# Where seven fill transfers stand on GpSimd in a two-layer cross-attention kernel

## The chip, the cores and the metric

The kernel runs on one core of one Trainium2 chip, in float32. A core has a matrix engine (TensorE, "PE" in the profile), a vector engine (VectorE, "DVE"), a scalar engine (ScalarE, "ACT"), GpSimd ("POOL") and SyncE ("SP"), and 16 DMA engines[...]. The metric is the device time of one execution in microseconds; lower is better. The median of three runs of the kernel before is 599.94 us (597.68 to 600.04).

## The reference

Two cross-attention layers over a batch of 8. The queries `x` have 100 rows of 1024 features per batch, the context has 1444 rows of 512.

```python
# layer 0
Q, K, V = query @ Wq + bq, key @ Wk + bk, key @ Wv + bv
weights = softmax(Q @ K.T / 32, axis=-1)              # over the 1444 context rows
x = query + (weights @ V) @ Wo + bo
# layer 1
q, k, v = x @ Wq + bq, ctx @ Wk + bk, ctx @ Wv + bv
w = softmax(q @ k.T / 32, axis=1)                     # over the 100 query rows
x = w @ v + x
out = (x - mean(x)) * rsqrt(var(x) + 1e-6) * gamma + beta
```

What matters for the change is the last line: `beta` is one row of 1024 numbers, and it is added to each of the 100 rows of each batch.

## The kernel before, in words

The kernel multiplies weights together first (`Wq` with `Wk`, `Wv` with `Wo`), so that the context is used as it comes from memory and never projected. It goes through these stages, in this order on the matrix engine:

1. Eight warm-up products (L111), then `qk0`, the product of layer 0's `Wq` and `Wk` (`weight_products`, L350). It is a Strassen-like scheme: the product is cut in quarters A11 to A22 and B11 to B22, and seven half-size products X, Z, W, Y and three more replace eight. X is A11 by B11, and Z is A12 by B21; both use the weights as loaded. W is A22 by T4, where `T4 = B21 - (B22 - (B12 - B11))` is made on VectorE. Y needs sums S1 and T1. The order on the matrix engine here is X, Z, W, Y and then products added to X.
2. `vo0` (`Wv` with `Wo`), the queries of layer 0, `qk1` (as `qk0`, for layer 1).
3. Layer 0's scores, softmax and weighted context rows, batch by batch (L913, L960), then its projection.
4. The queries of layer 1 and `key_bias_sums`, then layer 1's scores, softmax and weighted rows, its projection with `Wv` (loaded at L1380 into `wv1`), and the normalisation of each batch.

The weights of `qk0` come in eight tiles `qk0_0` to `qk0_7` ("units"), each with 1024 columns of transposed `Wq` and 512 of transposed `Wk`. Their loads are cut in halves and are issued in the order of use (L364 to L376): the two pieces of unit 0 on ScalarE's queue, and then, all on SyncE's queue, the first halves of `Wk` and `Wq` for all units (L368 to L371, 128 and 256 KB each), the second halves of `Wk` (L374, eight of 128 KB), and the second halves of `Wq` (L376, eight of 256 KB, units 4 to 7 first). Then come the loads of `vo0` (L379, L380). In the built program each of SyncE's transfers waits for the one eight places before it to have landed.

For all batches but the last, the result is put together by two kinds of transfers on GpSimd. A first one fills `out[b]` with 100 copies of `beta`'s row, straight from memory to memory (L1378; 400 KB each, seven of them). Much later `normalise` (L1234) makes the rest in a tile `z`, and a transfer that adds (L1247) puts it on top of what the fill left. The last batch doesn't use this.

The order of work is set in three ways. The matrix engine's instructions stand as they are written (`manual_schedule`). SyncE's loads in the batch loops (`loaded_in_order`), some activations and the vector operations with `in_order` are marked with `tc.keep_in_program_order`. All other instructions on the other engines are placed by the framework's scheduler, which may bring an instruction forward if nothing that it needs is missing. The fills read only an input and write only the output, so they need nothing: in the built program of the kernel before they stand right after the memset of `top` (L141), as the last of GpSimd's instructions before the first accumulating transfer of `qk0` (L578), though the source has them after the queries of layer 1.

Lines used further on: L130 (loads of bias columns), L141 (`top`), L166 (the products of `half_steps`), L440 (copies of finished products), L578 (accumulating transfers), L972 (memset in `scores_by_keys`), L1177 (last instruction of `weight_sums`), L185 (sums of `wv1` on GpSimd).

## Time and profile before

| | before |
|---|---|
| median of 3 runs | 599.94 us |
| profiled execution, its own time | 601.68 us |
| span of its instructions | 599.9 us |
| mean granted clock of the matrix engine | 0.991 |
| busy share: PE, DVE, POOL, ACT | 96%, 67%, 22%, 22% |
| moved by DMA | 142.96 MB, 6.14 MB of it written to memory |

How to read the profile: a row of a group names the source line, the engine, the operation, `output<-input` by the program's names (buffer and layer numbers left out, so that `qk0_4` is `qk`), the count, and the durations in microseconds or, where marked, nanoseconds. A time in brackets, as in `[3.49 <-DMA qk<-in_L_xattn_WkT]`, is how long the engine had stood idle before the instruction, and what ended this. In the profile of a window the columns are: start and end, length, then busy time of PE, PEld (weight loads), DVE, ACT and POOL, each with its instruction count in brackets, the granted clock of the matrix engine, the mean busy share of the 16 DMA engines, and GB/s.

### The profile page before, as it was taken

To read this page: it belongs to the slowest core of one execution; us is meant where nothing else is said; L and a number is where in the kernel's file an instruction comes from. 1 tells how busy PE (TensorE), PEld (TensorE's weight loads), DVE (VectorE), ACT (ScalarE), POOL (GpSimd) and SP (SyncE) were. 2 spreads that over 40 slices of the span, in tenths; PEclk is the share of its full clock that TensorE was granted. 3 is DMA by queue.
4 is the path that set the end of the run, shared out by engine and by line. 5 is a ranking of instruction groups with operands and counts; after the bars stand their busy time and mean duration, and the time that the engine had idled before them with its cause. 6 is when DMAs were issued, how large, how long until landed. Compare 5 with 4: busy or idle time off the path is not lost.

```text
span 599.9 us, 17567 instructions
## 1 busy us (share of the span) xinstructions
PE 578.0 (96%) x7470; PEld 498.5 (83%) x7470; DVE 399.7 (67%) x936; ACT 133.3 (22%) x349; POOL 134.9 (22%) x206
## 2 busy tenths in 40 slices
PE   8499999999999999999999999999999999999994
PEld 7378645768889999999998856677999999999992
DVE  1199758988867597284558688695644337664695
ACT  1032232131360002022200000112333203145313
POOL 5011011121120022252221100000931421332052
PEclk9889999999999999999999999999999999999998
DMA  8896998984379999899999201915799998499214
GB/s 253 238 295 136 311 299 216 328 201 99 71 158 323 322 393 357 295 379 364 365 341 296 96 0 63 380 55 162 244 292 334 336 301 294 117 315 320 68 29 83
DMA packets 74313, 142.96 MB, mean 238 GB/s; under 512 B 8572, under 2 KB 30332, under 8 KB 74236
## 3 DMA queue, kind: packets, MB, share of 16 engines
q1 hardware_dynamic: 65790, 117.81, 57.4%
q0 software_dynamic: 8048, 23.57, 18.8%
q8 instruction: 59, 0.97, 0.6%
q10 hardware_dynamic: 398, 0.47, 0.2%
q14 instruction: 18, 0.15, 0.1%
HBM read 124.40 MB, written 6.14 MB: 218 GB/s over the span
## 4 chain that ended last, share of the span: by engine, by line
PE 90%; DMA 4%; issue 2%; POOL 2%; ACT 1%; DVE 0%; SPq 0%; POOLq 0%; DVEq 0%
PE s L960 22%; PE A L913 21%; PE qk_x L166 6%; PE g_x L166 5%; PE o_x L166 5%; DMA qk<-in_L_xattn_WkT 4%; PE vo_x L166 3%; PE o_y L166 3%; PE g_y L166 3%; PE qk_y L166 2%; PE qk_w L166 1%; PE o_w L166 1%; PE o_z L166 1%; PE qk_z L166 1%; PE vo_z L166 1%
## 5 line engine op out<-in xcount | busy, mean ns | idle before, releaser
L913 PE MATMUL A<-w,c 128*64 128x100 f32 (+1 forms) x3072 | 228.1, 249 | 0.4 <-issue 0.4
L913 PEld LDWEIGHTS A<-w,c 128*64 128x64 f32 (+1 forms) x3072 | 200.4, 137 | 1.8 <-issue 1.4
L960 PE MATMUL s<-g0T,cT 128*64 128x100 f32 (+1 forms) x1472 | 113.0, 249 | 2.5 <-issue 2.4
L960 PE MATMUL s<-g1T,cT 128*64 128x100 f32 (+1 forms) x1472 | 113.8, 249 | 0.2 <-issue 0.2
L960 PEld LDWEIGHTS s<-g0T,cT 128*64 128x64 f32 (+1 forms) x1472 | 99.2, 136 | 5.0 <-issue 3.9
L960 PEld LDWEIGHTS s<-g1T,cT 128*64 128x64 f32 (+1 forms) x1472 | 97.1, 136 | 2.1 <-issue 1.6
L1172 POOL TENSOR_TENSOR part<-w 128x500 f32<-128x500 f32 x16 | 26.4, 1652 | 126.3 <-ACT w L1020 61.1
L1152 ACT ACTIVATE w<-w,negmax 128x100 f32<-128x100 f32 x96 | 34.9, 366 | 68.2 <-DVE negmax L99 68.2
L1020 ACT ACTIVATE w<-w 128x400 f32<-128x400 f32 (+2 forms) x32 | 12.0, 443 | 122.2 <-DVE w L99 122.2
L99 DVE SCALAR_TENSOR_TENSOR w<-s,kb 128x400 f32<-128x400 f32 (+2 forms) x32 | 13.9, 464 | 37.0 <-PE s L960 36.8
L99 DVE TENSOR_REDUCE most<-s 128x100 f32<-128x400 f32 (+1 forms) x24 | 12.5, 521 | 38.5 <-PE s L960 38.5
L166 PE MATMUL qk_x<-qk 128*128 128x256 f32 x128 | 30.0, 382 | 0.0
L166 PEld LDWEIGHTS qk_x<-qk 128*128 128x128 f32 x128 | 23.6, 192 | 3.0 <-ACT qk L440 0.2
L166 PE MATMUL qk_z<-qk 128*128 128x256 f32 x64 | 16.3, 409 | 8.0 <-DMA qk<-in_L_xattn_WkT 8.0
L166 PEld LDWEIGHTS qk_z<-qk 128*128 128x128 f32 x64 | 12.9, 206 | 11.0 <-issue 7.8
L972 POOL MEMSET w<- 68x100 f32 x16 | 3.8, 238 | 78.4 <-PE A L913 37.9
L1232 DVE SCALAR_TENSOR_TENSOR z<-vectors,r,z 100x512 f32<-100x512 f32 x16 | 11.4, 744 | 11.5 <-PE z L1230 11.3
L99 DVE TENSOR_TENSOR w<-w,rtotal 128x400 f32<-128x400 f32 (+2 forms) x32 | 18.2, 570 | 1.1
L1152 ACT ACTIVATION_READ_ACCUMULATOR w<-w,negmax 128x1 f32 x96 | 18.0, 188 | 0.0
L1245 ACT ACTIVATE z<-z,rstd 100x1024 f32<-100x1024 f32 x7 | 8.0, 1149 | 44.7 <-POOL rstd L1243 44.7
L578 POOL DMA_DIRECT2D qk_L_xattn_bk<-qk_L_xattn_bk x6 | 5.2, 925 | 56.3 <-ACT qk_L_xattn_bk L583 27.5
L99 DVE TENSOR_TENSOR xT<-xT,o_x 128x400 f32<-128x400 f32 (+1 forms) x32 | 16.0, 541 | 2.7 <-PE o_x L166 2.4
(435 smaller groups left out, 1048.1 us busy)
## 6 DMA issues: line engine op xcount, KB each, us to landing
c<-in_ctx SPq DMA_DIRECT2D x176, 256.0 KB
cT<-in_ctxT SPq DMA_DIRECT2D x96, 176.0 KB
cT<-in_ctxT SPq DMA_DIRECT2D x32, 370.0 KB
cT<-in_ctxT SPq DMA_DIRECT2D x32, 352.0 KB
cT<-in_ctxT SPq DMA_DIRECT2D x32, 194.0 KB
vo<-in_L_xattn_Wo SPq DMA_DIRECT2D x8, 512.0 KB
qk<-in_L_xattn_WqT SPq DMA_DIRECT2D x8, 512.0 KB
qk<-in_L_xattn_WqT SPq DMA_DIRECT2D x15, 256.0 KB
```

Of the source, the lines that this page charges most:

```text
L99: ins = getattr(nc.vector, op)(*args, **kw)
L166: nc.tensor.matmul(banks[n // per][:, n % per * width : (n % per + 1) * width], lhs[i][:, n * P : (n + 1) * P], rhs[i], start=(fresh and i ...
L578: nc.gpsimd.dma_start(out=to, in_=t, accum_op=ALU.add)
L913: nc.tensor.matmul(ps[h * HP : (h + 1) * HP, k * T : (k + 1) * T], c[m // CQ][:r, m % CQ, k * P + h * HP : k * P + (h + 1) * HP], w[:r, m, :],
L960: nc.tensor.matmul(to, cT[k][:, o : o + n], q[:, k, t0 : t0 + T], start=(k == 0 and m % GM == 0), stop=(k == LC - 1 or (k == LC - 2 and no ...
L972: nc.gpsimd.memset(s["w"][:PAD, MC - 1, :], 0.0)
L1020: nc.scalar.activation(rows, rows, AF.Exp)
L1152: nc.scalar.activation(rows[:, i, :], rows[:, i, :], AF.Exp, bias=negmax[:, i : i + 1], accum_out=total[:, i : i + 1])
L1172: add(part, w[:, 0:5, :], w[:, 5:10, :], ALU.add)
L1232: nc.vector.scalar_tensor_tensor(z[:, half], bv1[j][:T], s["r"], ps[:T, :], ALU.mult, ALU.add)
L1245: nc.scalar.activation(z, z, AF.Copy, scale=rstd)
```

## The change

The seven fill transfers are marked to keep their place in the program's order. Nothing is computed differently.

```diff
     run(more)
     vector.in_order = False
     for b in range(B - 1):
-        nc.gpsimd.dma_start(out=out[b], in_=a["L1_xattn_beta"].partition_broadcast(T))
+        rows = a["L1_xattn_beta"].partition_broadcast(T)
+        tc.keep_in_program_order(nc.gpsimd.dma_start(out=out[b], in_=rows))
     wv1 = weights.tile([P, LC, E], F32, tag="w", name="wv1")
     nc.gpsimd.dma_start(out=wv1, in_=a["L1_xattn_Wv"].rearrange("(c p) e -> p c e", p=P))
```

In the built program the seven transfers move, on GpSimd alone, from their place between the memset of `top` (L141) and the first L578 to a place right after the last L1177 of layer 0 (the sums of batch 7) and before the L972 memset of layer 1's batch 0 and the load of `wv1`. All other engines have the same instructions in the same order.

```diff
 L141 Memset top
-L1378 DMACopy out<-in_L_xattn_beta x7
 L578 DMACopy qk_L_xattn_bk<-qk_L_xattn_bk
 ...
 L1177 TensorTensor wsum<-wsum,w
+L1379 DMACopy out<-in_L_xattn_beta x7
 L972 Memset w
-L1380 DMACopy wv<-in_L_xattn_Wv
+L1381 DMACopy wv<-in_L_xattn_Wv
```

## The prediction

> **What bounds the kernel now.** I read the page's chain first, then who the matrix engine waited for, then its timeline where it waited, then the transfers.

> ```profile
> PE 90%; DMA 4%; issue 2%; POOL 2%; ACT 1%; DVE 0%; SPq 0%; POOLq 0%; DVEq 0%
> ...
> PE   8499999999999999999999999999999999999994
> PEclk9889999999999999999999999999999999999998
> ```

> These are the chain that ended last, and the busy and clock rows of the 40 slices of 15 us. The matrix engine sets the time from about 30 us to the end; a 4% share (24 us) is DMA, and only slice 2 (15 to 30 us) has a PE that is half idle. So a shift of its later work to an earlier time should come out at the end in full. The waits of PE:

> ```profile
> PE qk_z L166 <- DMA qk<-in_L_xattn_WkT: 8.0, 3, 3.6
> PE s L960 <- issue: 2.6, 6, 0.7
> PE qk_w L166 <- DVE qk_t L99: 2.1, 1, 2.1
> ```

> All the long ones are in the first product `qk0`. Its timeline from 10 to 32 us:

> ```profile
> 11.75 1.89 PE L166 MATMUL qk_z<-qk 128*128 128x256 f32 x8
> 17.13 1.97 PE L166 MATMUL qk_z<-qk 128*128 128x256 f32 x8 [3.49 <-DMA qk<-in_L_xattn_WkT]
> 22.66 3.38 PE L166 MATMUL qk_z<-qk 128*128 128x256 f32 x8 [3.56 <-DMA qk<-in_L_xattn_WkT]
> 27.00 1.99 PE L166 MATMUL qk_z<-qk 128*128 128x256 f32 x8 [0.96 <-DMA qk<-in_L_xattn_WkT]
> 31.08 1.10 PE L166 MATMUL qk_w<-qk_t,qk 128*128 128x256 f32 x4 [2.09 <-DVE qk_t L99]
> ```

> Each group of eight Z products needs one more unit of the weights, and units 5, 6 and 7 come some 5 us apart: 384 KB per 5 us, under 80 GB/s. The wait for `qk_t` is the same lack one step on: VectorE's first difference started at 27.81 after 18.5 us of waiting for the L374 halves. Who took the bandwidth:

> ```profile
> L1378 POOL DMA_DIRECT2D out<-in_L_xattn_beta x7: 537/544/582, 5.7 to 9.4; - x7
> ...
> DMA to landing us min/median/max: 9.7/14.1/18.1
> ```

> The fills are issued from 5.7 us and the last land near 27 us. The stage's windows (last columns: clock, DMA share, GB/s):

> ```profile
> 2.00:5.65 3.65, 3.65 (x18) 3.51 (x17) 1.23 (x2) 0.95 (x1) 3.56 (x8) 1.00 0.94 306
> 12.00:22.00 10.00, 3.61 (x16) 2.55 (x14) 0.00 (x0) 0.54 (x1) 0.00 (x0) 1.00 0.96 248
> 31.00:38.00 7.00, 6.92 (x24) 5.84 (x25) 7.00 (x14) 3.08 (x3) 0.58 (x1) 0.76 0.96 321
> ```

> Without fills the DMA engines move 306 and 321 GB/s; with them 248 at the same busy share, of which 7 x 0.41 = 2.87 MB are the fills'.

> [...] Here the two idle times of 3.49 and 3.56 us are followed by a clock of 0.50 at 23 to 25 us and at 33 to 35 us. [...]

> **What the removal at the start is worth.** Y begins at 39.75. Dense, 32 products of this shape take 6.91 us (Y itself: 39.75 to 46.66). Z starts at 11.75, so W would start at 18.66 and Y at 25.57: 14.18 us earlier. By parts: idle 3.49 + 3.56 + 0.96 + 2.09 = 10.10; slow clock 3.38 - 1.97 = 1.41 in the third Z group and 8.83 - 7.07 = 1.76 in W; 0.91 is the tail of a group's last product, which is hidden when the next follows.

> Can the loads keep that pace? I take 306 GB/s from 2.0 us, and 2.4 us from the last byte to the wait's end; both are estimates from rows, the second from an accumulating transfer of 256 KB that lands 3.3 us after issue, 0.86 us of which is its bytes. First halves of all units are 8 x 0.393 = 3.15 MB: landed at 2.0 + 10.3 + 2.4 = 14.7, needed for the last Z group at 16.9. With the L374 halves 4.19 MB: 18.1. The first A22 block (unit 4's L376) makes 4.46 MB: 19.0, needed at 18.66, so 0.3 late. The last A22 block, 5.24 MB: 21.5, needed at 23.9. The last of all, 6.29 MB: 25.0, needed as S1's last sum before 30.8.

> VectorE: its first difference could start at 15.1. T4's first piece is ready 1.8 us after the start (27.81 to 29.64 now), at 16.9; the last is held by the 18.1 and about 1.4 us of work, 19.5. Its two additions of Z (0.64 each) follow, and S1's first sum is done near 23, 2.5 us before Y. Now it is done at 36.1, 3.6 us before Y. The cover is thinner, but it is there; without it Y would slip by the missing part alone.

> After Y nothing that sets the pace is tied to the clock on the wall: `vo0`'s loads past two units wait for tiles that the `qk0` products free, and DMA share falls to 0.4 to 0.5 at 45 to 55 us, so the next full stretch of DMA starts earlier by the same amount. Gain: 14.18 - 0.3 = 13.9 us.

> **What the new place costs.** The seven issues take 7 x 0.544 = 3.8 us of GpSimd. Around that place:

> ```profile
> 332.22 0.39 POOL L1177 TENSOR_TENSOR wsum<-wsum,w 36x100 f32<-36x100 f32 x1
> 343.01 0.18 POOL L972 MEMSET w<- 68x100 f32 x1 [10.40 <-issue]
> 370.35 0.83 POOL L1380 DMA_DIRECT2D wv<-in_L_xattn_Wv  x1 [27.16 <-PE o_x L166]
> ```

> Queued behind are the L972 memset and the `wv` load. GpSimd stands idle for 10.4 us before the first and 27.2 us before the second, so the issues cost nothing, and even at 1.5 us each (10.4 / 7) they would not delay the memset. If they did, that tile is next written by layer 1's softmax after its scores, which begin at 403.9. The bytes:

> ```profile
> 335.00:345.00 10.00, 10.00 (x194) 9.11 (x191) 5.65 (x9) 0.00 (x0) 0.18 (x1) 1.00 0.01 3
> 345.00:370.35 25.35, 25.35 (x84) 15.23 (x83) 21.75 (x53) 0.00 (x0) 0.00 (x1) 1.00 0.00 0
> ```

> DMA is idle for 35 us there. The fills need 2.87 MB / 0.3 = 10 us alone, 21 us at the crawl of the start. Ahead of them SyncE's queue ends its prefetch at 331.3 and then waits for buffers until 379.8. The L1247 additions, which need the fills landed, begin at 519.8. Cost between 0 and 0.5 us; I take 0. L578 no longer stands behind the fills, but it waited for ScalarE until 37.4, so this is worth nothing of its own.

> Sum: span 599.9 - 13.9 = 586.0. The profiled execution took 601.68, 1.7 above the median; its span stands at the median, so the same subtraction gives 586.0 for the median.

> **Rivals.**
> - *The weights' own stream becomes the bound.* If the rate without fills stayed at the 242 GB/s of 11.75 to 31.08 us, the first A22 block lands at 2.0 + 18.4 + 2.4 = 22.8, 4.1 late, and such a gap brings the slow clock (1.8) again: gain 14.18 - 5.9 = 8.3, 591.6 us. [...] Against: 306 and 321 GB/s in both windows without fills.
> - *Hidden anyway: SyncE's issue sets the pace.* Its eight L374 issues took 15 us. If that were its own doing, nothing changes: 599.9. Against: each takes 0.33 us at the median, and what it waits for are landings.
> - *Slower: the fills make `wv` late.* `wv` is issued at 370.4 and lands 9.9 us later; GpSimd's sums of it (L185) start at 419.3, and the matrix engine reads it first at 492.8, or 478.9 when shifted. Fills from 318.6 would have to last 478.9 - 9.9 - 318.6 = 150 us, 19 GB/s, before PE waits, 164 us to eat the gain, and 167 us to give 603. They had 134 GB/s (2.87 MB in 21.4 us) in the worst crowd of the kernel.
> - *The change does nothing*: excluded by the built order.

> **How the numbers follow.** Full shift (584.5 to 588) 0.72; partly, the stream bounds (588 to 595) 0.18; more than the dense sum, below 584.5 (a later stage also runs freer) 0.04; no change 0.04; slower 0.02. About 0.5% (3 us) is what a measurement of this kernel can tell from no change. Faster 0.94, same 0.04, slower 0.02. The range 583.0 to 591.6 takes in the partial rival's worked value and a run to run spread of 2 us, and leaves out its worse half and the last two cases.

> **What would show it.** After: no PE idle over 1 us and no clock below 1 before 40 us; Y near 25.6 to 26.2; VectorE's first difference near 15; the fills at about 318.6 in an empty DMA; everything between with its old durations. A gap ahead of W with DMA share 1 is the first rival; a PE wait for DVE there means VectorE's cover was too thin; a Y at 26 but an end later than 588 means that a later stage gave time back.

## The result, and the profile after

The changed kernel takes 592.06 us in the median of 6 runs (589.33 to 593.25), the kernel before, in runs beside it, 598.61 us (596.71 to 600.04, 6 runs). The ratio is 0.9883 with a 95% interval of 0.9848 to 0.9918: faster by about 6.5 us, less than half of the 13.9 us that were predicted.

The profiled execution took 589.33 us with a span of 587.6. Its start looks as predicted. Four rows of PE's timeline from 0 to 50 us, the products X, Z, W and Y, answer to the ones with the four gaps:

```profile
4.64 8.31 PE L166 MATMUL qk_x<-qk 128*128 128x256 f32 x32
12.79 7.07 PE L166 MATMUL qk_z<-qk 128*128 128x256 f32 x32
19.70 7.07 PE L166 MATMUL qk_w<-qk_t,qk 128*128 128x256 f32 x32
26.60 7.07 PE L166 MATMUL qk_y<-qk_s 128*128 128x256 f32 x32
```

No row behind the warm-up products has an idle time in brackets, and Y begins at 26.60 instead of 39.75. The waits of PE over the whole execution, which answer to the ones shown of before:

```profile
PE s L960 <- issue: 1.9, 3, 0.7
PE A L913 <- issue: 1.7, 1, 1.7
```

The waits for the weights are gone, but there is a new one of 1.7 us, put down to "issue", which means that PE waited for nothing that the profile shows. GpSimd's timeline around the new place of the fills (start, busy time, engine, line, operation, tiles, shapes, number; in brackets the idle time before it and what ended it):

```profile
317.12 0.39 POOL L1177 TENSOR_TENSOR wsum<-wsum,w 36x100 f32<-36x100 f32 x1
317.46 3.85 POOL L1379 DMA_DIRECT2D out<-in_L_xattn_beta  x7
329.89 0.18 POOL L972 MEMSET w<- 68x100 f32 x1 [8.58 <-issue]
357.23 0.80 POOL L1381 DMA_DIRECT2D wv<-in_L_xattn_Wv  x1 [27.17 <-PE o_x L166]
```

PE's timeline of the changed kernel in the same stretch (excerpt):

```profile
319.32 7.77 PE L913 MATMUL A<-w,c 128*64 128x100 f32 x175
328.74 1.03 PE L913 MATMUL A<-w,c 128*64 128x100 f32 x17 [1.65 <-issue]
329.88 2.96 PE L166 MATMUL o_x<-A0T,vo 128*128 128x400 f32 x8
332.67 2.85 PE L166 MATMUL o_y<-o_t,o_s 128*128 128x400 f32 x8
```

GpSimd issues the fills in 3.85 us and nothing behind them is late, as predicted. But PE, which is at batch 7's weighted rows (192 matmul records, 8.46 us without a break in the kernel before), stops for 1.65 us with 17 records left, while the fills move.

Another part of the shortfall does not show in this trace: the profiled execution of before, from which the gain was worked out, was a long one. That is taken up below.

### The profile page after: what moved, and what is told of

Same layout as the page of the kernel before. It is cut to its first block, busy times and chain, and to the rows that moved or that the text cites. A ratio compares the mean times of both kernels' runs of the same rounds, so it can differ in the third digit from the quotient of the medians.

```text
span 587.6 us, 17570 instructions
## 1 busy us (share of the span) xinstructions
PE 575.2 (98%) x7470; PEld 497.6 (85%) x7470; DVE 399.6 (68%) x936; ACT 133.3 (23%) x349; POOL 135.0 (23%) x206
## 4 chain that ended last, share of the span: by engine, by line
PE 86%; DMA 6%; SPq 2%; issue 2%; POOL 2%; ACT 1%; DVE 0%; POOLq 0%; DVEq 0%
PE s L960 18%; PE A L913 17%; PE qk_x L166 7%; PE g_x L166 6%; PE o_x L166 5%; PE vo_x L166 4%; DMA cT<-in_ctxT 3%; PE o_y L166 3%; PE g_y L166 3%; DMA c<-in_ctx 3%; PE qk_z L166 2%; PE qk_y L166 2%; SPq L861 2%; PE o_w L166 1%; PE o_z L166 1%
## 5 line engine op out<-in xcount | busy, mean ns | idle before, releaser
L960 PE MATMUL s<-g0T,cT 128*64 128x100 f32 (+1 forms) x1472 | 112.7, 249 | 2.0 <-issue 1.9
L960 PE MATMUL s<-g1T,cT 128*64 128x100 f32 (+1 forms) x1472 | 114.1, 249 | 0.1
L960 PEld LDWEIGHTS s<-g1T,cT 128*64 128x64 f32 (+1 forms) x1472 | 97.7, 136 | 2.6 <-issue 1.8
L960 PEld LDWEIGHTS s<-g0T,cT 128*64 128x64 f32 (+1 forms) x1472 | 96.8, 136 | 3.4 <-issue 2.7
L99 DVE SCALAR_TENSOR_TENSOR w<-s,kb 128x400 f32<-128x400 f32 (+2 forms) x32 | 13.9, 463 | 37.5 <-PE s L960 37.3
L99 DVE TENSOR_REDUCE most<-s 128x100 f32<-128x400 f32 (+1 forms) x24 | 12.5, 520 | 36.5 <-PE s L960 36.5
L166 PE MATMUL qk_x<-qk 128*128 128x256 f32 x128 | 31.0, 392 | 0.0
L166 PEld LDWEIGHTS qk_x<-qk 128*128 128x128 f32 x128 | 24.3, 198 | 3.3 <-ACT qk L440 0.2
L972 POOL MEMSET w<- 68x100 f32 x16 | 3.8, 237 | 75.3 <-PE A L913 36.4
L99 DVE TENSOR_TENSOR w<-w,rtotal 128x400 f32<-128x400 f32 (+2 forms) x32 | 18.3, 570 | 1.1
L1152 ACT ACTIVATION_READ_ACCUMULATOR w<-w,negmax 128x1 f32 x96 | 18.1, 188 | 0.0
L99 DVE TENSOR_TENSOR xT<-xT,o_x 128x400 f32<-128x400 f32 (+1 forms) x32 | 15.9, 538 | 2.8 <-PE o_x L166 2.4
L674 ACT ACTIVATE g1T<-g_x,k 128x400 f32<-128x400 f32 x4 | 2.4, 594 | 61.4 <-PE g_x L166 61.2
L578 POOL DMA_DIRECT2D qk_L_xattn_bk<-qk_L_xattn_bk x6 | 5.2, 922 | 47.8 <-DMA qk_L_xattn_bk<-qk_L_xattn_bk 18.9
L166 PE MATMUL vo_x<-vo 128*128 128x512 f32 x32 | 15.3, 595 | 0.0
```

Of the source, the lines that this page charges most:

```text
L99: ins = getattr(nc.vector, op)(*args, **kw)
L166: nc.tensor.matmul(banks[n // per][:, n % per * width : (n % per + 1) * width], lhs[i][:, n * P : (n + 1) * P], rhs[i], start=(fresh and i ...
L578: nc.gpsimd.dma_start(out=to, in_=t, accum_op=ALU.add)
L960: nc.tensor.matmul(to, cT[k][:, o : o + n], q[:, k, t0 : t0 + T], start=(k == 0 and m % GM == 0), stop=(k == LC - 1 or (k == LC - 2 and no ...
L972: nc.gpsimd.memset(s["w"][:PAD, MC - 1, :], 0.0)
L1152: nc.scalar.activation(rows[:, i, :], rows[:, i, :], AF.Exp, bias=negmax[:, i : i + 1], accum_out=total[:, i : i + 1])
```

## The experiments

The kernel before differs by some us from chip to chip (medians of 598.1, 600.2 and 598.9 us in the three sets of runs below), so ratios compare better than times.

**The same two kernels again, without fills, and with the fills a little later.** The first question was whether the new place costs something, and how much. The changed kernel, two variants of it and the kernel before ran on one chip. The first variant leaves the fills out, so that seven batches of its output lack `beta`. The second holds them back behind a copy of one column that needs the last weighted rows of batch 7. In the cuts from the sources, the first is against the kernel before and the second against the changed kernel.

> The changed kernel once more, for the spread of its times and a second trace. Theory A (the fills at their new place hold up the fetch of the matrix engine's instructions during batch 7's weighted rows[...]): times from 589 to 593 us, and the trace has an idle time of PE put down to issue, of 1 to 5 us, between 318 and 332 us, while the fills move[...]. Theory B (the spread is the start's or the chip's): no such gap, and PE loses its time elsewhere. Theory C (start only, the profile of the kernel before was a slow one): the same times as with no fills at all.

> The changed kernel without the seven fills (the output of seven batches lacks beta; all else is done). Theory A: 586 to 588 us in every run, with little spread, and no PE idle time between 300 and 335 us; the difference to the changed kernel is the price of the new place, 2 to 5 us. Theory B: the same spread and median as the changed kernel, within 1 us. Theory C: the same as the changed kernel.

```diff
-    for b in range(B - 1):
-        rows = a["L1_xattn_beta"].partition_broadcast(T)
-        tc.keep_in_program_order(nc.gpsimd.dma_start(out=out[b], in_=rows))
```

> The changed kernel with the fills held back by about 13 us: a one-column copy on GpSimd that reads the last weighted rows of batch 7 stands before them, so that they run while PE does the long products of the projection. Theory A: as without fills, 586 to 588 us, PE dense from 318 to 345 us although the fills take as long there. Theory B and C: as the changed kernel, 589 to 593 us.

```diff
+    gate = const.tile([P, 1], F32, tag="gate", name="gate")
+    tc.keep_in_program_order(nc.gpsimd.tensor_copy(gate, A0[1][:, LC - 1, GT - 1 : GT]))
     for b in range(B - 1):
```

> The kernel before once more, for a second trace. All theories: 596 to 601 us; PE waits of 8 to 13 us in all before Y, and Y begins at 36 to 40 us. If its time is nearer 597 than 601, the start's loss should be smaller by the same 3 to 4 us[...].

| | median (range), us | ratio to before, interval |
|---|---|---|
| before, all runs on this chip | 598.12 (594.3 to 602.2) | |
| before again | 598.14 (596.18 to 600.01) | 0.9999 (0.9976 to 1.0021) |
| changed | 590.33 (588.84 to 592.35) | 0.9867 (0.9839 to 0.9895) |
| changed, no fills | 587.40 (585.30 to 588.05) | 0.9808 (0.9780 to 0.9837) |
| fills after batch 7's rows | 586.85 (585.93 to 588.48) | 0.9814 (0.9788 to 0.9840) |

So the new place costs 590.33 - 587.40 = 2.9 us (with six runs on each side, uncertain by about 2 us), and 14 us further on the same transfers cost nothing that can be seen: theory A. The second trace of the kernel before has PE waits of 1.55 + 4.60 + 0.77 = 6.9 us ahead of Y, less than the 8 to 13 that were expected; its Y begins at 38.14, as expected. The traces say where the 2.9 us are. PE's timeline in the second trace of the changed kernel:

```profile
317.75 7.77 PE L913 MATMUL A<-w,c 128*64 128x100 f32 x175
327.88 1.27 PE L913 MATMUL A<-w,c 128*64 128x100 f32 x17 [2.36 <-issue]
...
329.42 4.19 PE L166 MATMUL o_x<-A0T,vo 128*128 128x400 f32 x8
```

PE's timeline in the kernel with the fills held back until after batch 7's rows:

```profile
320.97 8.46 PE L913 MATMUL A<-w,c 128*64 128x100 f32 x192
...
329.53 2.95 PE L166 MATMUL o_x<-A0T,vo 128*128 128x400 f32 x8
332.32 2.85 PE L166 MATMUL o_y<-o_t,o_s 128*128 128x400 f32 x8
```

GpSimd's timeline of that kernel:

```profile
331.11 0.59 POOL L1378 COPY gate<-A0T 128x1 f32<-128x1 f32 x1 [1.38 <-DVE A0T L942]
331.64 3.85 POOL L1381 DMA_DIRECT2D out<-in_L_xattn_beta  x7
```

In the second trace of the changed kernel the stop is 2.36 us, at the same place, and the eight o_x records after it take 4.19 us instead of 2.95. The table of windows of that second trace shows a lower clock there (start and end, length, the busy times of PE, PEld, DVE, ACT and POOL, and last the clock, the DMA share and GB/s):

```profile
326.00:330.00 4.00, 2.12 (x22) 1.80 (x23) 0.48 (x1) 0.00 (x0) 0.18 (x1) 0.82 0.90 212
330.00:334.00 4.00, 4.00 (x10) 2.15 (x9) 3.83 (x8) 0.00 (x0) 0.00 (x0) 0.76 0.13 42
```

The clock is 0.82 in the stretch in which the stop ends (at 327.88) and 0.76 in the next. With the fills held back both stretches have 4.00 us of PE and a clock of 1.00.

**What PE stops for.** The profile has two DMA queues of kind "instruction", the larger of them q8 (59 packets, 0.97 MB). The 17 records come close to those of the last block of context rows (16), whose first product has waits in the program, so a wait on data that the profile doesn't name could not be excluded. If PE waits instead for its own instructions to come in (the fetch of theory A; that q8 carries them was at this point the author's guess from its kind), the place must move when instructions are put ahead of all others.

> The changed kernel with twelve tiny products (2 by 2 results) after the warm-up, which put 24 more matmul records into the matrix engine's stream ahead of everything. In both traces of the changed kernel the idle time in batch 7's weighted rows ended with 17 matmul records left of 192, with no wait named. Instruction fetch: the place moves with the stream, so the gap ends with 41 left (17 + 24). A wait on data (the 17 are about those of the last block of context rows, which also has a wait in the program): it stays at 17 or 16. Time within 2 us of the changed kernel's 589 to 593.

```diff
     for _ in range(8):
         nc.tensor.matmul(warm[:, :P], ones, ones, start=True, stop=True)
+    for _ in range(12):
+        nc.tensor.matmul(warm[:2, :2], ones[:, :2], ones[:, :2], start=True, stop=True)
```

The cut is against the changed kernel; each of the twelve products makes two matmul records. It took 591.37 us (2 runs; before on this chip 600.15). PE's timeline in that kernel:

```profile
322.17 6.74 PE L915 MATMUL A<-w,c 128*64 128x100 f32 x151
330.29 2.02 PE L915 MATMUL A<-w,c 128*64 128x100 f32 x41 [1.38 <-issue]
```

41 records are left, 24 more than in the changed kernel, just as many as were put in front. A wait on data would have stayed. The DMA view of the changed kernel from 326 to 327 us shows a packet of q8 among the fills (queue and kind, packets, MB, share of 16 engines):

```profile
q0 software_dynamic: 69, 0.22, 101.6%
q8 instruction: 1, 0.02, 7.6%
```

All 59 packets of q8 are of 16 KB, and the page counts their time, 0.7% in the changed kernel, as a share of the same 16 DMA engines as that of the fills. The trace doesn't name the engine that a packet on q8 is for, but the counts do. From 240 to 270 us PE starts 1,406 matmuls and weight loads in the changed kernel, and five packets move; from 340 to 385 us it starts 335, and one moves; in the whole execution it is 14,940 to 59. So q8 follows PE, with a packet for 14,940 / 59 = 253 of these on average.

The count of instructions gives the place of the stop as well. PE has started 7,874 instructions (matmuls, weight loads and its own semaphore instructions) when it goes on, in all four traces of the changed kernel and also in the one with the shifted stream. The 13 traces of this document have 60 stops of PE over 0.25 us in the batch products. Of these, 58 stand a multiple of 256 instructions from 7,874, to within one record, and each of them ends 2.2 to 2.8 us after a packet on q8 has started. (The other two are taken up below, with the fills in the batch loop.) Five stops of the kernel before, of 0.40 to 0.74 us and put down to "issue", are among the 58. By these counts and times the stops are waits for the next packet of PE's instructions.

The DMA view in steps of 0.5 us shows when such packets move after the start of batch 7's rows. Without fills the rows start at 320.97 and a packet moves in 323.0 to 323.5, 2.0 us or a little more later; in the kernel before they start at 334.42 and the packet moves in 336.0 to 336.5. In the changed kernel they start at 319.3, and the first packet after that moves only in 326.0 to 326.5, 6.7 us or a little more later; in the second trace it is 7.7 (317.8 to 325.5). The packet itself takes no longer, about 1 us (11.6% to 15.2% of 16 engines for 0.5 us), so it is its start that comes 4 to 6 us late. Why it starts late while the fills move, no run here shows. With the fills held back no packet falls due among them: q8 moves at 328.8 us and next at 362, and the fills move from 333 to 347.

**Two more traces of the changed kernel**, for its longer executions, and a second run of the best version.

> The changed kernel, a third trace. The span from Y's first product to the end was 560.1 us in both traces of the kernel before, and 561.0 and 562.0 in the two of the changed kernel. Fetch theory: an idle time that ends with 17 records of batch 7 left, 1.5 to 4 us, and the span from Y on is 560.1 plus this gap plus what a slow clock adds after it, less what the batch loop's own issue gaps differ (about 1 us). If the slower executions (591 to 593 us) lose their time elsewhere, a trace with a span over 589 us shows no larger gap there.

> The changed kernel, a fourth trace. As for the third: an idle time with 17 records of batch 7 left, and a span from Y on that is longer than 560.1 us by about that gap and the slow clock after it.

> The version with the fills held back until batch 7's weighted rows are done, on another chip, against the kernel before: ratio 0.979 to 0.984 (0.9814 on the first), and no idle time of PE between 318 and 345 us.

The third execution took 591.06 us, the fourth 589.92. Both stop with 17 records left, as expected. The table measures the traces from Y's first product on, and from the start of batch 7's rows to `o_y`, the second product behind them, by which the clock is back at 1.00 in all of them:

| trace | Y begins | span | Y to the end | Y to batch 7's rows | rows to `o_y` | stop in the rows |
|---|---|---|---|---|---|---|
| before | 39.75 | 599.9 | 560.15 | 294.67 | 11.36 | none |
| before again | 38.14 | 598.2 | 560.06 | 294.53 | 11.36 | none |
| changed, 1st | 26.60 | 587.6 | 561.00 | 292.72 | 13.35 | 1.65 |
| changed, 2nd | 25.19 | 587.2 | 562.01 | 292.57 | 15.69 | 2.36 and slow clock |
| changed, 3rd | 25.31 | 589.3 | 563.99 | 292.92 | 15.88 | 2.56 and slow clock |
| changed, 4th | 25.03 | 588.1 | 563.07 | 292.86 | 15.55 | 2.23 and slow clock |
| no fills | 26.54 | 586.0 | 559.46 | 294.43 | 11.36 | none |
| fills after batch 7's rows | 26.60 | 586.7 | 560.10 | 294.37 | 11.36 | none |
| the same, again | 25.75 | 584.7 | 558.95 | 292.34 | 11.36 | none |

From the rows to `o_y` it is 11.36 us wherever the fills are not among the rows, and 2.0 to 4.5 us more in the changed kernel: this is what the stop costs in these four executions, slow clock included. They were also 1.5 to 2 us quicker between Y and the rows than four of the other five. That is not the new place's doing, since the last trace, which has no fills there, is as quick; what decides it is open. It hides a part of the stop's cost in the sum from Y to the end, and the 2.9 us of the medians are the better figure for the change as a whole.

In its two traces the kernel before varies ahead of Y, where it waits for its weights, and hardly after it. The best version repeated at 586.39 us against 598.93 (ratio 0.9808, 0.9761 to 0.9854), with no stop. Two of its six runs took 590.2 and 592.2, though; no trace shows what they lost.

**Other places.** Three more kernels on one chip (before: 600.15, 23 runs) asked what a place needs.

> The fills near the start, but after the weights: a one-column copy on GpSimd that waits for ScalarE's copy of Y stands before them, so they run from about 33 us, where DMA share is 0.3 to 0.55 and PE's products are long. If only the collision with qk0's weights costs: as without fills, 586 to 589 us. If the fills then collide with vo0's loads, which fill DMA from 45 us: PE waits in vo0, 590 to 597.

```diff
         put(1, 1, Y)
+        if name == "qk0":
+            gate = const.tile([P, 1], F32, tag="gate", name="gate")
+            tc.keep_in_program_order(nc.gpsimd.tensor_copy(gate, dst[:, l_width // P - 1, r_width - 1 : r_width]))
+            for b in range(B - 1):
+                rows = a["L1_xattn_beta"].partition_broadcast(T)
+                tc.keep_in_program_order(nc.gpsimd.dma_start(out=out[b], in_=rows))
```

The loop at its old place is gone. 593.89 us, ratio 0.9917 (0.9881 to 0.9953). The fills were issued from 35.2 us on and the last landed at 54.7, and then `vo0` waited for its weights, from 59 us on. The waits of PE in that kernel:

```profile
PE vo_x L166 <- DMA vo<-in_L_xattn_Wo: 2.8, 1, 2.8
...
PE vo_z L166 <- DMA vo<-in_L_xattn_Wo: 1.5, 1, 1.5
```

In the changed kernel these two waits are not there, and its DMA share is 0.30 from 30 to 35 us and 0.55 from 35 to 40. So DMA engines that were half idle for some 10 us were not free for the fills here: they took 19.5 us, and `vo0`'s loads behind them came 2.76 and 1.47 us late. This is the second of the two expectations.

> The fills later still, by program order after layer 1's first scores: GpSimd reaches them at about 425 to 435 us, in the batch loop, where PE's instructions are short and many (350 matmul records in 15 us) and DMA is 0.8 to 1.0 busy with context rows. Fetch theory: issue gaps of PE of 1 to 5 us in all between 425 and 455 us, 588 to 593. If fetch has nothing to do with it: 586 to 588.

Here the three lines of the loop stand after `run(scores1)`. It took 596.24 us, ratio 0.9936 (0.9903 to 0.9968): worse than either expectation. GpSimd issued the fills from 419.5 us on, and the last landed at 440.0. The waits of PE in that kernel:

```profile
PE s L960 <- DMA cT<-in_ctxT: 6.9, 3, 3.4
PE s L960 <- issue: 2.4, 3, 1.2
```

The profile puts most of this down to the context's columns (`cT`), but one of the three waits is something else. PE's timeline at that place, and q8 in the DMA view from 435.0 to 435.5 us:

```profile
437.39 0.31 PE L960 MATMUL s<-g1T,cT 128*64 128x100 f32 x2 [3.20 <-DMA cT<-in_ctxT]
q8 instruction: 1, 0.02, 11.6%
```

The instruction there does wait for a transfer of `cT` in the program. But of the transfers on its semaphore one had landed by 423.7, and the next had its last part at 439.7, after PE had gone on. The place is 2,304 = 9 x 256 instructions behind 7,874, and PE goes on 2.25 us after the packet has started. So this is a stop for instructions, of 3.2 us, as the first expectation has it, and the clock is 0.56 in the 3.6 us after it. The second long wait, 3.43 us at 474.27, is for `cT`: the last part of that transfer landed at 474.23. Such a wait is in none of the other traces; that the fills had set these loads back is likely, but not shown. It was not expected, and with it the run is slower than the 593 of the first expectation.

> Three fills at the old early place, four at the free place after batch 7. By bytes, 3/7 of the start's loss of 10.7 us comes back: 591.5 us. If the loss has a threshold (the loads have some slack), less: 587 to 590.

```diff
+    for b in range(3):
+        nc.gpsimd.dma_start(out=out[b], in_=a["L1_xattn_beta"].partition_broadcast(T))
+    gate = const.tile([P, 1], F32, tag="gate", name="gate")
+    tc.keep_in_program_order(nc.gpsimd.tensor_copy(gate, A0[1][:, LC - 1, GT - 1 : GT]))
-    for b in range(B - 1):
+    for b in range(3, B - 1):
```

The cut is against the changed kernel. 593.65 us, ratio 0.9890 (0.9861 to 0.9918). Against 0.9814 with all seven late this is 0.0076 x 600 = 4.6 us, and 3/7 of 10.7 is 4.6. So the start's loss going by the bytes fits, but the intervals of the two ratios leave 2 to 7 us, and the comparison is across chips: slack in the loads is made less likely, not excluded. The trace is of the shortest run (590.07) and has two waits ahead of Y, 1.38 and 0.76 us, with Y at 28.69, some 2 to 4 us later than without fills there.

## Why the prediction was wrong

The direction was right, and so was the mechanism of the gain at the start. Two terms of the sum were mis-sized: the gain in a usual execution, and the cost of the new place, which was put at nothing. By the prediction's own steps:

- **The removal at the start, in the trace: right.** Y was to begin at 25.6 to 26.2; it began at 26.60, 25.19, 25.31 and 25.03. Idle times and slow clock before it are gone (the clock is 1.00 from 0 to 30 us in the first two traces). VectorE's first difference was estimated for 15.1 and came at 13.95; PE never waited for VectorE between X and Y. The 26.60 has a first product X of 8.15 us instead of 6.91; the kernel before shows such an X too (7.8 in its second trace), so this is not the change's.
- **The step from one execution to the median: wrong.** The prediction said of the profiled execution of before that "its span stands at the median". It compared a span of 599.9 with times that have 1.75 us around their spans, and had three runs. With more runs the kernel before takes 598.1 to 598.9, a span of about 596.5, so the execution that was profiled was some 3.4 us longer than usual. Since the two traces of before agree after Y (560.15 and 560.06), the excess most likely lies in the start's waits: the very term that was summed. A usual Y is then at about 36.4 (worked out, not traced). Measured on the medians, the removal is worth 598.12 - 587.40 = 10.7 us with no fills, and 11.3 and 12.5 with the fills held back, on two chips (598.12 - 586.85, 598.93 - 586.39): not 13.9.
- **"Cost between 0 and 0.5 us; I take 0": wrong, it is 2.9 us.** GpSimd's issues, the memset behind them and the `wv` load came out as said (3.85 us; 8.58 us and 27.17 us still idle). The bytes did too, nearly: the fills were issued from 317.5 us, and the last landed at 333.9. What the step left out is a reader of the DMA engines that is no tile's load: PE's instructions. In batch 7's rows PE runs through them fast (164 matmul and 166 weight load records in 7.0 us from 319.4 us on, against 168 and 167 in the 45 us from 340 on), and there the packets that started 4 to 6 us late stopped it for 1.65 to 2.56 us.
- On that chip the two terms are 10.7 and 2.9, and 598.12 - 590.33 = 7.8 was gained. That they add up is no further proof, since both are differences to the same kernel without fills. The first comparison gave 6.5; the intervals of the two ratios overlap.
- **The signs.** The one for a later stage that gives time back, a Y at 26 but an end later than 588, is what the third and fourth traces show (Y at 25.31 and 25.03, spans of 589.3 and 588.1); the first two traces ended ahead of 588 in spite of the stop.
- **The rivals.** The weights' own stream did not become the bound, and `wv` was not late. (The slow clock of 1.8 us in that rival's sum was an estimate of the author's from W's 1.76; in the second trace of the kernel before, eight Z products took 3.78 us instead of 1.97 after a wait of 4.60.) The measured 592 lies in the band from 588 to 595, which the prediction gave to that stream with 0.18; that the band was hit is chance. The true rival was a price at the new place, and it was not on the list.
- **A reading of the clock was wrong**, without weight in the sum. The prediction has the clock of 0.50 at 23 to 25 and at 33 to 35 us follow the idle times of 3.49 and 3.56 us. After the first of them the clock is 1.00 (the eight products at 17.13 take 1.97 us); the slow stretch at 33 to 35 follows the wait of 2.09 us ahead of W. So here a clock of 0.50 came after idle times of 3.56 and 2.09 us, and 1.00 after one of 3.49.

The page of before held the hint, in its table of queues and in PE's waits: a queue of kind "instruction" with 59 packets, and waits put down to "issue" in the batch loop (2.6 us in six places), where the DMA share is 1.01 (195 to 310 us). The prediction shows the line of these waits but asks nothing about it.

## What to carry to other kernels

A transfer that waits for nothing can be placed anywhere by a scheduler, and here it stood where it was cheap for its own engine. Look at what the DMA engines carry at that place: among the loads of `qk0`'s weights the seven fills cost 10.7 us. When such a transfer is moved, look for three things at the new place, each of which went with a loss here: loads in flight (the same 10.7 us), loads that follow without slack (waits of 2.8 and 1.5 us in `vo0`), and a stretch where an engine runs through its instructions fast (stops of 1.65 to 2.56 us in batch 7's rows). The long products right after batch 7's rows showed none of the three and gave 586.9 us, better than both kernels. If an engine stops with no wait named, or with a wait for something that landed long before or later, count its instructions up to the stop in several traces: here the stop that stayed at 7,874, and moved by 24 records when 24 were put in front, was the one for instructions. And before a sum made from one trace is set against a median, see where that one execution stands among the runs, span against span.
